# A depthwise convolution and a GRU over 256 steps: another order of channels on the partitions, and what follows from it for loads and products

## The chip, the cores and the metric

The kernel runs on one core of a Trainium2 chip. The metric is the device time of one execution in microseconds, the median of several runs. All times of the profile come from one profiled execution of the kernel before.

## The reference

Inputs: `x` of 16 x 256 x 512 (batch, time, channel), `cond` of 16 x 512, and the weights and biases of a GRU (`W_ih`, `W_hh` of 512 x 1536, gates in the order r, z, n). All is float32.

```
def _L0_cond_ref(x, w):              # causal depthwise convolution, K = 16 taps over time
    return conv_general_dilated(x, w, window_strides=(1,), padding=[(K - 1, 0)],
                                dimension_numbers=('NHC', 'HIO', 'NHC'), feature_group_count=C)

def cell(h, x):                      # GRU step, scanned over 256 steps
    gi = x @ W_ih + b_ih;  gh = h @ W_hh + b_hh
    r = sigmoid(i_r + h_r);  z = sigmoid(i_z + h_z)
    n = tanh(i_n + r * h_n)
    return (1 - z) * n + z * h

x = x + _L0_cond_ref(x, cond[:, None, :])        # x1; cond is the convolution's weight
out = x1 + scan(cell, initial_state=cond, x1)    # the states of all steps are added to x1
```

So `cond` serves as the 16 taps of the convolution and as the GRU's first state. The 256 steps of the GRU depend on each other; the products `x1 @ W_ih` do not.

## The kernel before

**Layout.** A channel c (0 to 511) lies on partition p = 32j + l in slot q, with j = c // 128, and within that block of 128 channels q = column // 32 and l = column % 32: `by_part` cuts 128 columns as `(q l)`. State, `x1T`, `xT` and `ni` stand in this transposed form [128, 4, ...]; the recurrent products put the gates into the natural form, with row 32j + batch and 128 columns of block j, and VectorE turns them back with transposes of 32x32 blocks (`rnT` L449, `zp` L461, `xT` L222, the output at L522), reading or writing 32 neighbouring columns for one block.

**Loads.** `load_weights` (L171 to L178) fetches a gate's 512 x 512 weights (for r and z of `W_ih` 512 x 1024) by four transfers, each to the 32 partitions of one j. Two queues, SP and POOL, issue them, after the two first chunks of x. The weights of the recurrent products (`whh`, gates R, N, Z) are issued last (L579 to L582).

**Start.** TensorE clears banks (`mark`, L350 and L351: bf16 products on the full array), then runs `PAD` = 108 idle products of 32 columns and one moving column (L356), and drains. Of chunk 0 (16 steps of x), slots q = 2 and 3 are convolved on TensorE by 16 products each with a diagonal matrix that ScalarE makes (`conv_on_tensor`, L288 to L300; 128 stationary columns, float32), and slots 0 and 1 on VectorE tap by tap (L265). Then come the biases (`spread_biases`, L362), the candidate's x1 products for the first 8 steps (`ni_units`, L320), r and z's x1 products for the first two steps (`pair_units`, L383), and part of chunk 1's taps on VectorE (`bulk.run(0, HEAD)`).

**A step** (`step`, L403 on) issues on TensorE, in this order: 16 products for r (L418, tile `prz`), 16 for n (L418, `pnh`), 16 for z (L418, `prz`), then `other_products`: two units of `pair_units` (8 products, moving 256 columns) and two units of `ni_units` (8 products). All of these have 16 or 32 stationary columns and go to one of four column groups of the array, j = 0 to 3; the four of a kc run side by side. A float32 product is recorded as two instructions in the profile. Of one unit of `ni_units` the before kernel says:

```
for j in range(NQ):
    nc.tensor.matmul(
        hold[q][32 * j : 32 * j + 32, 0:n],
        lhsT=wih_n[:, kc, j * P + q * L : j * P + q * L + L],
        rhs=x1T[c][:, kc, o : o + n], ...
```

One block of 8 steps has 16 such units, spread over the 8 steps before it. Beside that the other engines make the step's chain: r's sigmoid on ScalarE (L435), `rn` (L447), `rnT` (L449), `n` (L451) on VectorE, tanh on ScalarE (L459), `zp` (L461), sigmoid of z (L465), the difference (L467) and a scan (L474) that writes the new state `hist` for the next step's products for r. VectorE also does the taps of later chunks (L265), as many in each step as a plan (`Plan`, due steps and costs) asks, and the sums for the output.

The changed kernel's line numbers are lower by 3 to 12: its products of the step stand at L413, those of `ni_units` at L316.

Of the kernel before, what the change touches and what calls it, by code (L numbers as in the profile page):

```python
# [24 lines left out]
F32 = mybir.dt.float32  # L25
BF16 = mybir.dt.bfloat16
AF = mybir.ActivationFunctionType
# [3 lines left out]
P = 128  # L31
# [3 lines left out]
CHUNKS = (16,) * 16  # L35
PAD = 108
HEAD = 11.0
SYNC = mybir.DependencyInfo(mybir.DependencyClass.Sync, mybir.DependencyReason.DATA)
# [37 lines left out]
def conv_gru_kernel(  # L76
# [36 lines left out]
    def by_part(natural):  # L113
        return natural.rearrange("p (q l) -> p q l", q=NQ)

# [24 lines left out]
    for j in range(NQ):  # L140
# [12 lines left out]
    nc.vector.memset(ones, 1.0)  # L153
    bn_nat = const.tile([P, P], F32)
    nc.vector.memset(bn_nat, 0.0)

    load_x(1, ((nc.sync,), (nc.gpsimd,)))
    nc.sync.dma_start(out=b_two[0:1, :], in_=b_hh.rearrange("(o c) -> o c", o=1))
    nc.sync.dma_start(
        out=b_two[1:2, 0 : 2 * C], in_=b_ih[0 : 2 * C].rearrange("(o c) -> o c", o=1)  # L160
    )
    nc.gpsimd.dma_start(
        out=bn_nat[0:P:L, :], in_=b_ih[2 * C : 3 * C].rearrange("(j c) -> j c", j=NQ)
    )

# [4 lines left out]

    def load_weights(w_sb, w, g, queues):  # L171
        for j in (0, 2, 1, 3):
            queues[j].dma_start(
                out=w_sb[L * j : L * j + L],
                in_=w[j * P : (j + 1) * P, g * C : g * C + w_sb.shape[2]].rearrange(
                    "(q l) c -> l q c", l=L
                ),
            )  # L178


    for tile_of, g in ((wih_n, N), (wih_rz, R)):
        load_weights(tile_of, w_ih, g, (nc.sync, nc.sync, nc.gpsimd, nc.gpsimd))
    zero_z = [const.tile([P, NQ * B * 2], F32, name=f"zero_z_{i}") for i in range(2)]
# [11 lines left out]
    bnT = const.tile([P, NQ, L], F32)  # L195

# [15 lines left out]
    def turn_units(c):  # L212

        def halo():
            xT[c] = xtp.tile([P, NQ, HALO + CMAX], F32, tag="xT", name=f"xT_{c}")
            if c:
                m = CHUNKS[c - 1] * B
                nc.scalar.copy(xT[c][:, :, 0:HALO], xT[c - 1][:, :, m : m + HALO])

        def turn(a):  # L220
            o = HALO + a * PAIR
            nc.vector.transpose(  # L222
                xT[c][:, :, o : o + GT * B].rearrange("p q (a r) -> p a q r", r=L),
                x_nat[c][:, a : a + GP].rearrange("p a (q l) -> p a q l", q=NQ),
            )
# [79 lines left out]
    def ni_units(t0, steps):  # L305
# [6 lines left out]
        def prod(q, kc):  # L312
# [4 lines left out]
            if kc == 0:  # L317
                hold[q] = ps_ni.tile([P, NI * B], F32, tag="pni", name=f"pni_{t0}_{q}")
            for j in range(NQ):
                nc.tensor.matmul(  # L320
                    hold[q][32 * j : 32 * j + 32, 0:n],
                    lhsT=wih_n[:, kc, j * P + q * L : j * P + q * L + L],
                    rhs=x1T[c][:, kc, o : o + n],
                    start=(kc == 0),
                    stop=(kc == NQ - 1),
                    skip_group_check=True,
                )
            if kc == NQ - 1:
                evictions.append(lambda: evict(q))

        def evict(q):
            nc.scalar.activation(  # L332
                hold["ni"][:, q, 0:n], hold[q][:, 0:n], AF.Identity, bias=bnT[:, q, 0:1]
            )
# [18 lines left out]
    def idle_products(n):  # L353

        for _ in range(n):
            nc.tensor.matmul(  # L356
                spare[0:L, 0, 0:1], lhsT=blank[:, 0:L], rhs=blank[:, 0:1], start=True, stop=True
            )
# [136 lines left out]
    def out_units(g, a0=0, a1=GP, steps=(0, 1), queues=(nc.sync,)):  # L495
# [24 lines left out]
        def store():  # L520
            t = op.tile([P, GP, P], F32, tag="o", name=f"o_{g}_{a0}_{steps[0]}")
            nc.vector.transpose(  # L522
                t[:, 0:w].rearrange("p a (q l) -> p a q l", q=NQ),
                hold["s"][:, 0:w],
# [27 lines left out]
    for q in range(NQ):  # L552
        if q not in Q_PE:
# [3 lines left out]
                last1[:, q : q + 1],  # L557
            )
    conv_on_tensor()

    taps = [fn for i, (_, fn) in reversed(list(enumerate(tap_units(0)))) if i % NQ not in Q_PE]
    needed = (NI - 1) * (NQ - len(Q_PE))
    for fn in taps[:needed]:
        fn()
    for _, fn in turn_units(1):
        fn()
    nc.vector.transpose(bnT, by_part(bn_nat))
    for fn in taps[needed:]:
        fn()
    evictions.pop(0)()  # L570
    first_terms(1)
    give_firsts()
    evictions.pop(0)()
    spread_biases()
    nc.scalar.copy(b_rows, spare)
    seed_rz(0)
    seed_nh(0)
    seed_rz(1)
    for g in (R, N, Z):  # L579

        second = nc.sync if g == Z else nc.gpsimd
        load_weights(whh[g], w_hh, g, (nc.sync, second, nc.gpsimd, nc.gpsimd))  # L582
    for fn in ni_units(*blocks[0]):
# [7 lines left out]
    for c in range(1, NCH):  # L591
        due = starts[c] - NI
        taps = tap_units(c)
# [12 lines left out]
    for t in range(T):  # L606
# [6 lines left out]
        def other_products():  # L613

            for units in (of_pair, of_block):
                for _ in range(2):
                    if units:
                        units.pop(0)()
# [54 lines left out]
```

## Time and profile before

| | |
|---|---|
| median of 3 runs | 1043.28 us (1041.05, 1043.28, 1046.07) |
| span of the profiled execution | 1039.8 us |
| PE (TensorE matmul) busy | 1022.6 us, 98% |
| DVE (VectorE) busy | 926.8 us, 89% |
| ACT (ScalarE) busy | 380.3 us, 37% |
| first recurrent product, and that of the second step | 27.95 us, 36.33 us |
| one step of the GRU, once it runs | 3.92 us |
| moved by DMA in the first 36 us | 7.45 MB |

The profiled execution has no time of its own beside its span; the median of the runs stands 3.5 us above that span, and this is taken for what lies around it.

The chain of waits follows the execution back from its last instruction and says which work ended last at each point. Groups give, for all instructions of one line and shape, the count, the busy time, the mean duration of one and the idle time before them. The timeline lists instructions in order of time; neighbours of one group are merged, so that a row gives the start of the first, the time to the end of the last, and how many. Ends of matmuls are modelled: a matmul of 128 moving columns is drawn with 273 ns, though another can start 27 ns after it. The pace of TensorE is therefore read from starts, not from durations. PEld is the loading of weights into the array, which normally runs ahead of the product that needs it.

### The profile page before, as it was taken

The numbers are of one execution on the slowest core, as the hardware profiler recorded it, in microseconds if no ns is written. First come the engines' busy times: TensorE is split into PE (matmuls) and PEld (weight loads), VectorE is DVE, ScalarE is ACT, GpSimd is POOL, SyncE is SP. The second block draws the span as 40 slices with busy tenths as digits, with TensorE's granted clock in tenths as the row PEclk, the third lists the DMA queues.
The fourth block names the chain that finished last, engine by engine and source line by source line (L and its number), as shares of the span: only waits on it lengthen the run. The fifth ranks groups of instructions, "written<-read, shape, count | busy, mean of one in ns | idle before, by whom it ended". The sixth has DMA issues, their size and how long they took to land.

```text
span 1039.8 us, 71852 instructions
## 1 busy us (share of the span) xinstructions
PE 1022.6 (98%) x32952; PEld 928.5 (89%) x32952; DVE 926.8 (89%) x3606; ACT 380.3 (37%) x1520; POOL 12.4 (1%) x29
## 2 busy tenths in 40 slices
PE   7899999999999999999999999999999999999997
PEld 6699999999999999999999999999999999999986
DVE  7899999999999999999999999999999999896555
ACT  6233433334333333433334333343433334333332
POOL 4000000000000000000000000000000000000000
PEclk9999999999999999999999999999999999999999
DMA  9420101101010010100100010010000000000000
GB/s 216 111 58 13 26 15 29 21 15 31 8 35 14 15 35 8 32 15 19 30 14 26 14 34 15 15 34 5 15 14 15 15 13 6 15 15 15 14 11 17
DMA packets 40850, 27.72 MB, mean 27 GB/s; under 512 B 6686, under 2 KB 38498, under 8 KB 40548
## 3 DMA queue, kind: packets, MB, share of 16 engines
q1 hardware_dynamic: 38756, 18.78, 8.0%
q8 instruction: 257, 4.21, 1.7%
q0 software_dynamic: 1376, 4.20, 1.7%
q14 instruction: 45, 0.37, 0.1%
q10 hardware_dynamic: 416, 0.16, 0.1%
HBM read 14.73 MB, written 8.39 MB: 22 GB/s over the span
## 4 chain that ended last, share of the span: by engine, by line
PE 95%; DMA 3%; DVE 1%; SPq 0%; issue 0%; ACT 0%; DVEq 0%; ACTq 0%
PE prz L418 42%; PE pnh L418 21%; PE prz L383 20%; PE pni L320 10%; DMA whh<-in_L_cond_W_hh_dram 2%; DMA x_nat<-in_x_dram 1%; DVE rnT L449 0%; DVE zp L461 0%; DVE rn L447 0%; SPq L125 0%; ACT zero_z L465 0%; DVE n L451 0%; DMA out_dram<-o 0%; DVE hist L474 0%; DVE glance L398 0%
## 5 line engine op out<-in xcount | busy, mean ns | idle before, releaser
L418 PE MATMUL prz<-whh,hist 128*32 128x128 f32 x16320 | 539.9, 273 | 3.0 <-DVE hist L474 2.1
L418 PEld LDWEIGHTS prz<-whh,hist 128*32 128x32 f32 x16320 | 450.0, 103 | 8.5 <-DVE hist L474 6.6
L265 DVE SCALAR_TENSOR_TENSOR x1T<-xT,condT,x1T 128x256 f32<-128x256 f32 (+2 forms) x930 | 377.4, 462 | 0.0
L418 PE MATMUL pnh<-whh,hist 128*32 128x128 f32 x8160 | 269.7, 273 | 0.0
L383 PE MATMUL prz<-wih_rz,x1T 128*32 128x256 f32 x4096 | 268.2, 379 | 0.1
L418 PEld LDWEIGHTS pnh<-whh,hist 128*32 128x32 f32 x8160 | 226.7, 104 | 0.0
L459 ACT ACTIVATE dn<-n 128x64 f32<-128x64 f32 x256 | 67.9, 265 | 325.9 <-DVE n L451 325.9
L383 PEld LDWEIGHTS prz<-wih_rz,x1T 128*32 128x32 f32 x4096 | 129.0, 110 | 43.7 <-issue 0.3
L320 PEld LDWEIGHTS pni<-x1T,wih_n 128*32 128x32 f32 x4096 | 122.8, 110 | 42.7 <-ACT x1T L300 0.6
L435 ACT ACTIVATE r<-prz 128x128 f32<-128x128 f32 x256 | 71.1, 278 | 238.6 <-PE prz L418 235.5
L320 PE MATMUL pni<-x1T,wih_n 128*32 128x128 f32 x4096 | 158.1, 273 | 0.0
L474 DVE TENSOR_TENSOR_SCAN hist<-zero_z,dn 128x32 f32<-128x32 f32 (+1 forms) x768 | 128.6, 216 | 0.0
L447 DVE TENSOR_TENSOR rn<-r,pnh 128x128 f32<-128x128 f32 x256 | 72.4, 283 | 38.5 <-PE pnh L418 37.2
L465 ACT ACTIVATE zero_z<-zp 128x32 f32<-128x32 f32 x512 | 90.6, 226 | 8.6 <-DVE zp L461 1.8
L449 DVE STREAM_TRANSPOSE rnT<-rn 128x128 f32<-128x128 f32 x256 | 79.7, 311 | 8.7
L461 DVE STREAM_TRANSPOSE zp<-prz 128x128 f32<-128x128 f32 x256 | 80.9, 316 | 1.8 <-PE prz L418 1.7
L332 ACT ACTIVATE ni<-pni,bnT 128x128 f32<-128x128 f32 x128 | 47.1, 368 | 74.7 <-PE pni L320 74.7
L467 DVE TENSOR_TENSOR dn<-hist,dn 128x64 f32<-128x64 f32 x255 | 58.4, 229 | 11.3
L451 DVE TENSOR_TENSOR n<-rnT,ni 128x64 f32<-128x64 f32 x256 | 57.7, 225 | 8.9
L398 DVE COPY glance<-r 1x1 f32<-1x1 f32 x256 | 34.0, 133 | 25.3 <-ACT r L435 25.3
L371 ACT COPY prz<-b_rows 128x256 f32<-128x256 f32 x128 | 48.5, 379 | 0.0
L398 DVE COPY glance<-zero_z 1x1 f32<-1x1 f32 x256 | 36.3, 142 | 8.0 <-ACT zero_z L465 0.3
(51 smaller groups left out, 211.1 us busy)
## 6 DMA issues: line engine op xcount, KB each, us to landing
out_dram<-o SPq DMA_DIRECT2D x248, 32.0 KB, 1.7
x_nat<-in_x_dram SPq DMA_DIRECT2D x118, 64.0 KB, 3.0
whh<-in_L_cond_W_hh_dram POOLq DMA_DIRECT2D x8, 256.0 KB, 14.7
wih_rz<-in_L_cond_W_ih_dram POOLq DMA_DIRECT2D x2, 512.0 KB, 10.2
wih_rz<-in_L_cond_W_ih_dram SPq DMA_DIRECT2D x2, 512.0 KB, 14.3
whh<-in_L_cond_W_hh_dram SPq DMA_DIRECT2D x4, 256.0 KB, 19.0
x_nat<-in_x_dram POOLq DMA_DIRECT2D x8, 64.0 KB, 5.4
wih_n<-in_L_cond_W_ih_dram POOLq DMA_DIRECT2D x2, 256.0 KB, 7.7
```

The costliest lines, as they stand in the source:

```text
L265: nc.vector.scalar_tensor_tensor(out=x1T[c][:, q, to], in0=xT[c][:, q, k * B + to.start : k * B + n], scalar=condT[:, q, k : k + 1], in1=x ...
L320: nc.tensor.matmul(hold[q][32 * j : 32 * j + 32, 0:n], lhsT=wih_n[:, kc, j * P + q * L : j * P + q * L + L], rhs=x1T[c][:, kc, o : o + n], ...
L383: nc.tensor.matmul(rz[p % 2][32 * j : 32 * j + 32], lhsT=x1T[c][:, kc, o : o + PAIR], rhs=w_rz[:, :, j * P : (j + 1) * P], start=False, st ...
L398: nc.vector.tensor_copy(glances[i][0:1], of_scalar[0:1, 0:1])
L418: product = nc.tensor.matmul(dst[32 * j : 32 * j + m], lhsT=h[0](kc), rhs=whh[g][:, kc, j * P : (j + 1) * P], start=False, stop=(kc == NQ ...
L435: of_r = nc.scalar.activation(r, pr, AF.Sigmoid)
L447: nc.vector.tensor_mul(rn, r, pnh)
L449: nc.vector.transpose(rnT, by_part(rn))
L459: nc.scalar.activation(dn_v[:, :, :, 1], n, AF.Tanh)
L461: nc.vector.transpose(zp, by_part(pz))
L465: nc.scalar.activation(z_v[:, qs, :, 1], zp[:, qs, half], AF.Sigmoid) for qs in halves
L474: nc.vector.tensor_tensor_scan(hist_g[:, lo + at : lo + end], z[:, to], dn[:, to], 0.0, op0=ALU.mult, op1=ALU.add,)
```

## The change

Channel 4p + q lies on partition p in slot q: `by_part` cuts 128 columns as `(l q)`, so a 32x32 block to transpose takes every fourth column. With it:

- `load_weights` fetches a gate by two transfers of all 128 partitions, slots 0 and 1 by SP and 2 and 3 by POOL; `whh` is issued right after `W_ih`, and chunk 1 of x after the candidate's weights. The candidate's bias comes by one transfer in place of a load and a transpose.
- A unit of `ni_units` is one product with 128 stationary columns, every fourth of `wih_n`, on the full array, in place of four with 32.
- The idle products are 200 with 40 moving columns (108 with one before); `spread_biases` and the seeds come before the convolution, and chunk 0's taps on VectorE are no longer interrupted by the turn of chunk 1.
- `HEAD` is 7.0 instead of 11.0, chunk 1 is due two steps later, and the units for steps 16 to 23 begin two steps later.

```diff
-PAD = 108
-HEAD = 11.0
+PAD = 200
+IDLE = 40
+HEAD = 7.0
...
     def by_part(natural):
-        return natural.rearrange("p (q l) -> p q l", q=NQ)
+        return natural.rearrange("p (l q) -> p q l", q=NQ)
...
-    load_x(1, ((nc.sync,), (nc.gpsimd,)))
...
+    nc.sync.dma_start(out=bnT, in_=b_ih[2 * C : 3 * C].rearrange("(p q) -> p q", q=NQ))
...
-    def load_weights(w_sb, w, g, queues):
-        for j in (0, 2, 1, 3):
-            queues[j].dma_start(
-                out=w_sb[L * j : L * j + L],
-                in_=w[j * P : (j + 1) * P, g * C : g * C + w_sb.shape[2]].rearrange(
-                    "(q l) c -> l q c", l=L
-                ),
-            )
-
-    for tile_of, g in ((wih_n, N), (wih_rz, R)):
-        load_weights(tile_of, w_ih, g, (nc.sync, nc.sync, nc.gpsimd, nc.gpsimd))
+    def load_weights(w_sb, w, g):
+        rows = w.rearrange("(p q) c -> p q c", q=NQ)
+        for queue, qs in ((nc.sync, slice(0, NQ // 2)), (nc.gpsimd, slice(NQ // 2, NQ))):
+            queue.dma_start(
+                out=w_sb[:, qs], in_=rows[:, qs, g * C : g * C + w_sb.shape[2]]
+            )
+
+    load_weights(wih_n, w_ih, N)
+    load_x(1, ((nc.sync,), (nc.gpsimd,)))
+    load_weights(wih_rz, w_ih, R)
+    for g in (R, N, Z):
+        load_weights(whh[g], w_hh, g)
...
-                x_nat[c][:, a : a + GP].rearrange("p a (q l) -> p a q l", q=NQ),
+                x_nat[c][:, a : a + GP].rearrange("p a (l q) -> p a q l", q=NQ),
...
-            for j in range(NQ):
-                nc.tensor.matmul(
-                    hold[q][32 * j : 32 * j + 32, 0:n],
-                    lhsT=wih_n[:, kc, j * P + q * L : j * P + q * L + L],
-                    rhs=x1T[c][:, kc, o : o + n],
-                    start=(kc == 0),
-                    stop=(kc == NQ - 1),
-                    skip_group_check=True,
-                )
+            nc.tensor.matmul(
+                hold[q][:, 0:n],
+                lhsT=wih_n[:, kc, q:C:NQ],
+                rhs=x1T[c][:, kc, o : o + n],
+                start=(kc == 0),
+                stop=(kc == NQ - 1),
+            )
...
-                spare[0:L, 0, 0:1], lhsT=blank[:, 0:L], rhs=blank[:, 0:1], start=True, stop=True
+                spare[0:L, 0, 0:IDLE], lhsT=blank[:, 0:L], rhs=blank[:, 0:IDLE], start=True, stop=True
...
-                t[:, 0:w].rearrange("p a (q l) -> p a q l", q=NQ),
+                t[:, 0:w].rearrange("p a (l q) -> p a q l", q=NQ),
...
+    spread_biases()
     conv_on_tensor()
-
-    taps = [fn for i, (_, fn) in reversed(list(enumerate(tap_units(0)))) if i % NQ not in Q_PE]
-    needed = (NI - 1) * (NQ - len(Q_PE))
-    for fn in taps[:needed]:
-        fn()
-    for _, fn in turn_units(1):
-        fn()
-    nc.vector.transpose(bnT, by_part(bn_nat))
-    for fn in taps[needed:]:
-        fn()
-    evictions.pop(0)()
-    first_terms(1)
-    give_firsts()
-    evictions.pop(0)()
-    spread_biases()
     nc.scalar.copy(b_rows, spare)
     seed_rz(0)
     seed_nh(0)
     seed_rz(1)
-    for g in (R, N, Z):
-        second = nc.sync if g == Z else nc.gpsimd
-        load_weights(whh[g], w_hh, g, (nc.sync, second, nc.gpsimd, nc.gpsimd))
+    taps = [fn for i, (_, fn) in reversed(list(enumerate(tap_units(0)))) if i % NQ not in Q_PE]
+    for fn in taps:
+        fn()
+    for _, fn in turn_units(1):
+        fn()
+    while evictions:
+        evictions.pop(0)()
+    first_terms(1)
+    give_firsts()
...
-        due = starts[c] - NI
+        due = starts[c] - NI + (2 if c == 1 else 0)
...
             for units in (of_pair, of_block):
-                for _ in range(2):
+                late_block = units is of_block and t // NI == 1
+                for _ in range(((0, 0, 2, 2, 3, 3, 3, 3)[t % NI]) if late_block else 2):
```

More of the change, by code (lines that the diff above doesn't have):

```diff
@@ L153, in conv_gru_kernel @@
     nc.vector.memset(ones, 1.0)
-    bn_nat = const.tile([P, P], F32)
-    nc.vector.memset(bn_nat, 0.0)
-    load_x(1, ((nc.sync,), (nc.gpsimd,)))
+    bnT = const.tile([P, NQ], F32)
     nc.sync.dma_start(out=b_two[0:1, :], in_=b_hh.rearrange("(o c) -> o c", o=1))
@@ L161, in conv_gru_kernel @@
     )
-    nc.gpsimd.dma_start(
-        out=bn_nat[0:P:L, :], in_=b_ih[2 * C : 3 * C].rearrange("(j c) -> j c", j=NQ)
-    )
+    nc.sync.dma_start(out=bnT, in_=b_ih[2 * C : 3 * C].rearrange("(p q) -> p q", q=NQ))
     wih_rz = const.tile([P, NQ, 2 * C], F32)
@@ L193, in prepare_cond @@
         nc.vector.tensor_scalar_add(last1, condT[:, :, K - 1], 1.0)
-    bnT = const.tile([P, NQ, L], F32)
     b_rows = const.tile([P, 3, P], F32)
@@ L332, in evict @@
             nc.scalar.activation(
-                hold["ni"][:, q, 0:n], hold[q][:, 0:n], AF.Identity, bias=bnT[:, q, 0:1]
+                hold["ni"][:, q, 0:n], hold[q][:, 0:n], AF.Identity, bias=bnT[:, q : q + 1]
             )
```

## The prediction

> **What bounds the kernel now.** First the page's shares of busy time and the chain of waits:
>
> ```profile
> PE 1022.6 (98%) x32952; PEld 928.5 (89%) x32952; DVE 926.8 (89%) x3606; ACT 380.3 (37%) x1520; POOL 12.4 (1%) x29
> PE 95%; DMA 3%; DVE 1%; SPq 0%; issue 0%; ACT 0%; DVEq 0%; ACTq 0%
> ```
>
> A busy PE alone proves little, since its ends are modelled, but the chain stays on PE for 95% of the span. Only the start differs: there the chain lies on DMA. The second question is how far the steps' other chain (VectorE, ScalarE) is behind. Two steps in the timeline tell it, one in the middle and one of the last eight, which have no candidate's x1 products (L320):
>
> ```profile
> 500.81 1.06 PE L418 MATMUL prz<-whh,hist 128*32 128x128 f32 x32
> 501.68 1.05 PE L383 MATMUL prz<-wih_rz,x1T 128*32 128x256 f32 x16
> 502.55 0.62 PE L320 MATMUL pni<-x1T,wih_n 128*32 128x128 f32 x16
> 502.62 0.50 DVE L474 TENSOR_TENSOR_SCAN hist<-zero_z,dn 128x32 f32<-128x32 f32 x3
> 502.98 0.29 PE L418 MATMUL prz<-whh,hist 128*16 128x128 f32 x3
> ...
> 1010.59 1.06 PE L418 MATMUL prz<-whh,hist 128*32 128x128 f32 x32
> 1011.47 1.05 PE L383 MATMUL prz<-wih_rz,x1T 128*32 128x256 f32 x16
> 1012.40 0.50 DVE L474 TENSOR_TENSOR_SCAN hist<-zero_z,dn 128x32 f32<-128x32 f32 x3
> 1012.66 0.61 PE L418 MATMUL prz<-whh,hist 128*16 128x128 f32 x13
> ```
>
> From the first product for z to the next step's first for r takes 2.17 us in the middle (0.87 for z, 0.87 for L383, 0.43 for L320, no gap) and 2.07 us at the end, where PE waits for the scan. So the vector chain alone would allow 2.07: it has 0.10 us of slack in a step. If the L320 products cost nothing, 246 steps would gain 246 x 0.10 = 25 us; anything added to them is paid in full.
>
> **The products on the full array.** A step has 8 products now, two groups of four side by side, 0.43 us. It will have two, each of 128 stationary columns. The convolution shows what such products cost in a row:
>
> ```profile
> 18.75 0.48 PE L292 MATMUL conv<-xT,diag 128*128 128x128 f32 x3
> ...
> 19.08 1.31 PEld L292 LDWEIGHTS conv<-xT,diag 128*128 128x128 f32 x11
> ```
>
> Less the last record's 0.26, three records span 0.22: a record each 0.11 us at 128 moving columns. Weight loads come each (1.31 - 0.19) / 10 = 0.112 us. A product is two records, so two products take 4 x 0.109 to 4 x 0.112 = 0.44 to 0.45 us: what they take now. Four column groups side by side already did the work of one full array, and a quarter of the instructions saves no time. I take +1 us over all steps (0 to +3).
>
> **The change of mode.** Before, a step stays with products of one column group throughout. Now L383 and the recurrent products use groups, and the two products between use the full array: two changes in a step. The trace has changes from full to groups, at the start:
>
> ```profile
> 1.72 0.31 PE L351 MATMUL pnh<-blank 128*128 128x128 bf16 x1
> ...
> 1.95 0.10 PEld L356 LDWEIGHTS <-blank 128*32 128x32 bf16 x1 [0.30 <-issue]
> 1.96 0.19 PE L356 MATMUL spare<-blank 128*32 128x1 bf16 x1
> ...
> 20.34 0.26 PE L292 MATMUL conv<-xT,diag 128*128 128x16 f32 x1
> 20.53 0.10 PEld L362 LDWEIGHTS spare<-b_two,ones 2*32 2x32 f32 x1
> 20.53 0.51 PE L362 MATMUL spare<-b_two,ones 2*32 2x384 f32 x1
> ```
>
> Elsewhere a load runs some 0.1 us ahead of its product. Here load and product start together, 0.19 us after the last full product where the pitch was 0.11, and 0.24 us after where it was 0.11: the array emptied first, for 0.08 to 0.13 us. The first product after a late load of 32 columns is drawn 24 ns longer (297 ns against a median of 273 in the answer on line L320). So a change to groups costs 0.08 + 0.02 = 0.10, up to 0.15 us. A change to the full array is not in the trace. The nearest rows bound it: from the same emptying with a covered load, 0.08 + 0.02 = 0.10, to 0.13 with a whole 128-column load in the open, 0.13 + 0.112 = 0.24. I take 0.08 + 0.112 = 0.19, since nothing loads ahead in either row. A gain is excluded: PE has no gap there to fill. Both: 0.29 us in a step, bounds 0.20 and 0.39. There are 30 blocks of 8 steps and one of 6 with such products, 246 steps: **246 x 0.29 = 71 us**, bounds 49 and 96. It is all on the path. The next product for r is queued behind it, and r's sigmoid, `rn` and the scan wait for that. The slack of 0.10 is on the other side: the vector chain becomes later than needed by 0.10 + 0.29 = 0.39 us.
>
> **Every fourth column.** `rnT` and `zp` (L449, L461), the turns of x (L222) and the output's transposes will step by 16 bytes. No DVE row here does; a step of 8 bytes, in the scan's output read by L467, costs nothing visible. 128 columns take 311 ns and 512 take 688: 0.98 ns per element. Unchanged is one bound; twice the rate per element is the other, 128 x 0.98 = 0.13 us for each of two transposes in the step's chain, 0.26 us together. Both lie within the 0.39 us that the slower PE leaves, so I take 0; without that cover they would cost (0.26 - 0.10) x 256 = 41 us. VectorE would be busy for 256 x 0.26 + 31 x 2 x 0.5 = 98 us more, 1025 us of a span of some 1105, still not the bound.
>
> The 128-column loads of `wih_n` step by 16 bytes too. Those of `hist` step by 8 and take 97 to 110 ns like the rest. Bounds: 0, or each load twice as long, 4 x 0.112 = 0.45 us in a step, 246 x 0.45 = 110 us. I take 0, as the nearest row does.
>
> On this the Trainium skill ("SBUF — State Buffer", Door 1: The DMA port swizzle) speaks against the change: SBUF has lines of 16 bytes, and full bandwidth needs at least two accesses to a line. A step of 16 bytes has one; by the rule the transposes and loads would lie near the slow bounds, which adds nothing for the transposes and up to 110 us for the loads. It also says that four float32 can be stepped for free, so it does not decide, and no row here does.
>
> **The start.** The chain waits for the recurrent weights: the first product for z begins at 34.20 us on landing, step 1 at 36.33.
>
> ```profile
> 11.42 22.65 DMA whh<-in_L_cond_W_hh_dram
> ...
> 14.00:21.50 7.50, 7.50 (x68) 6.77 (x70) 7.50 (x28) 3.04 (x8) 1.87 (x4) 1.00 1.03 307
> 21.50:24.00 2.50, 2.50 (x96) 2.30 (x92) 2.50 (x8) 1.97 (x6) 0.33 (x1) 1.00 1.04 211
> ```
>
> The last column is GB/s. The same busy queues move 307 in one stretch and 211 in another, with transfers to 32 partitions. From 9.5 to 34.0 us the table of stages holds 6.25 MB; at 307 GB/s all through that is 20.4 us and ends 4.1 us earlier, at the 344 of the best half microseconds 18.2 us and 6.3 earlier. I take 5; bounds 0 (if packets, not partitions, set the rate) and 6.3. PE follows: convolution done at 20.5 or before, 16 candidate's products by about 23, L383 (1.9 us) by 25, then the first product for r, 2 to 3 us before today's. VectorE follows with `HEAD` = 7: four units fewer in front; the due steps of chunk 1 keep its rate (18.5 units over 10 steps, 14.5 over 8 before).
>
> The idle products: the convolution's first slot took 6.6 us (9.37 to 15.96), the second, of the same sizes, 4.6. Column PEclk stands at 1.00 in both, so by it nothing is to be won; the pitch says that PE ran at half pace until about 13.6 us, after an idle stretch from 5 to 9.4. 200 products of 40 columns close most of that stretch: 2 us less for PE, hidden behind the weights' landing and counted in the 25 us above. The Trainium skill ("TensorE: Matmul & The Clock Gate", Part 1) has the clock halved after about 3.4 us of idleness, which agrees with the pitch and not with the column; by either the sum stays, as DMA ends last. `bnT` in 16-byte pieces, the one-transfer bias and the moved `spread_biases` are small and lie beside the loads: 0.
>
> **Sum.** 1039.8 (span) + 71 + 1 - 5 = 1106.8; with 3.5 around it as between span and median, **1110 us**. Its own bounds: 1043.3 + 49 + 0 - 6 = 1086 and 1043.3 + 96 + 3 = 1142.
>
> **Rivals.**
> 1. *The change of mode costs nothing* inside a stream of ready products; the gaps at the start would be start-up effects (one stands at 2 us, the other falls on two stationary rows too, which is another change). Then steps stay at 3.92 us and the start's gain is left: 1043.3 - 6.3 = 1037, at 5 us 1039. This is the case on the fast side; it decides if both changes together cost under 5 / 246 = 0.02 us. For it: two instances only, none in a step. Against it: two instances, and in both the load was not ahead. 28%.
> 2. *No emptying, but slow transposes*: VectorE's chain becomes the bound, 2.07 + 0.26 = 2.33 us against 2.17: 1043.3 + 41 - 5 = 1079. Nearly the same if only one change of two is paid: 246 x 0.10 = 25, 1063. 19%.
> 3. *The weight loads bind as well*: emptying plus 0.45 us in a step, 1110 + 110 = 1220. 7%.
> 4. Forecast, 1086 to 1142: 46%.
>
> Of rival 1, over three quarters lie under 1038. A measurement of this kernel can tell about 0.5% (5 us) from no change. Chances: faster 0.22, same 0.06, slower 0.72. The range, to hold eight in ten, must reach from rival 1 (with 3 us below it, the spread of the runs shown) over 2 to the forecast's upper bound: 1034 to 1142; the forecast alone is 1086 to 1142.
>
> **What would show it.** Right: in a step of the changed profile, the first L316 product starts some 0.19 us later after L378 than the pitch, with its load beside it and not ahead; the next L413 product 0.10 later; the step takes 4.2 us; PE still carries the chain. Wrong: steps of 3.92 us, and loads of L316 ahead of L378's end. Rival 2 shows as L449 and L461 at 0.44 us and PE waiting for the scan; rival 3 as loads of L316 with a pitch of 0.22 us. For the start: `whh` landed by 29 us, 300 GB/s or more throughout, the convolution's two slots alike at 4.6 us, and step 1 at 31 us.

## The result, and the profile after

The changed kernel takes 1246.8 us (1246.5 to 1246.9, four runs) against 1042.3 us for the kernel before in the same comparison: 1.196 times as long, 95% interval 1.194 to 1.199. The profiled execution took 1246.8 us, its span is 1245.0 us, 205.2 us more than before. That is slower, as forecast, but by three times the forecast's 67 us and outside its range.

The page's shares of busy time and its chain of waits, changed kernel:

```profile
PE 1232.1 (99%) x29972; PEld 1050.3 (84%) x29972; DVE 983.6 (79%) x3604; ACT 371.0 (30%) x1520; POOL 8.9 (1%) x21
PE 97%; DVE 1%; ACT 1%; issue 0%; ACTq 0%; DMA 0%; SPq 0%; DVEq 0%
```

PE issues 9% fewer instructions and is busy 209.5 us longer. Weight loads (PEld) are busy 122 us longer, although the candidate's 4096 loads of 32 columns became 1024 of 128. VectorE's share fell. DMA has left the chain: the start is PE's too.

One step in the timeline (columns: start, us, engine, line, operation, tile, sizes, count; rows that the reading doesn't need are left out, here and below), stationary loads and products:

```profile
599.90 1.05 PE L378 MATMUL prz<-wih_rz,x1T 128*32 128x256 f32 x16
600.88 1.01 PEld L316 LDWEIGHTS pni<-x1T,wih_n 128*128 128x128 f32 x4 [0.41 <-issue]
600.88 1.20 PE L316 MATMUL pni<-x1T,wih_n 128*128 128x128 f32 x4
600.89 0.52 DVE L469 TENSOR_TENSOR_SCAN hist<-zero_z,dn 128x32 f32<-128x32 f32 x3
602.01 1.07 PE L413 MATMUL prz<-whh,hist 128*16 128x128 f32 x32
```

Three things stand here. The first L316 load starts with its product and not ahead of it, after 0.41 us in which the load queue waits for nothing that the profile shows. The scan ends at 601.41, and the next step's products for r start only 0.6 us later (0.61 in the median of the steps): the vector chain no longer decides the end of a step. And the two L316 products, four records, stand from 600.88 to 602.01, 1.13 us, where the eight products took 0.43 us before.

The single records inside that line begin at 600.879, 601.215, 601.450 and 601.683: a pitch of 0.234 us, where contiguous 128-column loads have 0.11 (the convolution, in both kernels). The first distance is 0.336, that is 0.10 more. The last group of four L378 products starts at 600.55 and has streamed by 600.77, if it takes the 0.216 us that lie between the groups before it; by this estimate nothing streams for 0.11 us before the first load. The first L413 record comes 0.327 after the last L316 record, 0.09 more than the pitch.

A step takes 4.755 us in the mean of steps 10 to 245 (from one sigmoid of r to the next), 3.92 before. It splits into 3.49 for r, n, z and L378 as before, 4 x 0.234 = 0.94 for the records of L316, and 0.33 that remains for the two changes of mode (the gaps just read, 0.11 + 0.10 + 0.09, make 0.30 of it). Against before (0.43 for the eight products) that is +0.51 + 0.33; times 246 it is 125 + 81 = 206 us, and the span grew by 205.

### The profile page after: what moved, and what is told of

Read it like the earlier page. It is cut to its first block, busy times and chain, and to the rows that moved or that the text cites. A ratio compares the mean times of both kernels' runs of the same rounds, so it can differ in the third digit from the quotient of the medians.

```text
span 1245.0 us, 65870 instructions
## 1 busy us (share of the span) xinstructions
PE 1232.1 (99%) x29972; PEld 1050.3 (84%) x29972; DVE 983.6 (79%) x3604; ACT 371.0 (30%) x1520; POOL 8.9 (1%) x21
## 4 chain that ended last, share of the span: by engine, by line
PE 97%; DVE 1%; ACT 1%; issue 0%; ACTq 0%; DMA 0%; SPq 0%; DVEq 0%
PE prz L413 38%; PE pni L316 23%; PE pnh L413 18%; PE prz L378 17%; PE conv L289 1%; ACT diag L285 0%; DVE rnT L444 0%; DVE rn L442 0%; ACT dn L454 0%; DVE n L446 0%; DVE dn L462 0%; DVE hist L469 0%; DVE o L517 0%; DVE x1T L262 0%; DMA out_dram<-o 0%
## 5 line engine op out<-in xcount | busy, mean ns | idle before, releaser
L413 PE MATMUL prz<-whh,hist 128*32 128x128 f32 x16320 | 543.8, 274 | 4.5 <-DVE hist L469 4.5
L413 PEld LDWEIGHTS prz<-whh,hist 128*32 128x32 f32 x16320 | 430.3, 103 | 39.0 <-DVE hist L469 8.9
L316 PEld LDWEIGHTS pni<-x1T,wih_n 128*128 128x128 f32 x1024 | 257.6, 324 | 101.3 <-issue 100.9
L316 PE MATMUL pni<-x1T,wih_n 128*128 128x128 f32 x1024 | 304.8, 422 | 0.0
L413 PE MATMUL pnh<-whh,hist 128*32 128x128 f32 x8160 | 269.5, 273 | 0.0
L378 PE MATMUL prz<-wih_rz,x1T 128*32 128x256 f32 x4096 | 267.8, 379 | 0.0
L413 PEld LDWEIGHTS pnh<-whh,hist 128*32 128x32 f32 x8160 | 226.4, 104 | 0.0
L378 PEld LDWEIGHTS prz<-wih_rz,x1T 128*32 128x32 f32 x4096 | 127.9, 110 | 44.1
L469 DVE TENSOR_TENSOR_SCAN hist<-zero_z,dn 128x32 f32<-128x32 f32 (+1 forms) x768 | 131.9, 227 | 0.0
L444 DVE STREAM_TRANSPOSE rnT<-rn 128x128 f32<-128x128 f32 x256 | 108.6, 424 | 8.8
L219 DVE STREAM_TRANSPOSE xT<-x_nat 128x512 f32<-128x512 f32 x32 | 36.4, 1144 | 5.0 <-DMA x_nat<-in_x_dram 5.0
```

Of the source, the lines that this page charges most:

```text
L316: nc.tensor.matmul(hold[q][:, 0:n], lhsT=wih_n[:, kc, q:C:NQ], rhs=x1T[c][:, kc, o : o + n], start=(kc == 0), stop=(kc == NQ - 1),)
L378: nc.tensor.matmul(rz[p % 2][32 * j : 32 * j + 32], lhsT=x1T[c][:, kc, o : o + PAIR], rhs=w_rz[:, :, j * P : (j + 1) * P], start=False, st ...
L413: product = nc.tensor.matmul(dst[32 * j : 32 * j + m], lhsT=h[0](kc), rhs=whh[g][:, kc, j * P : (j + 1) * P], start=False, stop=(kc == NQ ...
L444: nc.vector.transpose(rnT, by_part(rn))
L469: nc.vector.tensor_tensor_scan(hist_g[:, lo + at : lo + end], z[:, to], dn[:, to], 0.0, op0=ALU.mult, op1=ALU.add,)
```

## The experiments

All times are compared with the kernel before on the same chip (1042 to 1044 us). In the short diffs, "after" is the changed kernel.

**1. Contiguous loads on the full array.** Theory A: stationary loads that step by 16 bytes take twice as long and set the pitch. Theory B: on the full array load and product take turns, whatever the step.

```
+    wih_np = const.tile([P, NQ, NQ, P], F32)
+    for kc in range(NQ):
+        nc.gpsimd.tensor_copy(wih_np[:, kc], wih_n[:, kc].rearrange("p (m q) -> p q m", q=NQ))
-                lhsT=wih_n[:, kc, q:C:NQ],
+                lhsT=wih_np[:, kc, q],
```

> The changed kernel, but GpSimd copies the candidate's weights once, at the start, so that the 128 columns of each load of the full-array products lie side by side. Theory A (every load of 128 columns at a step of 16 bytes takes twice as long and sets the pace; beside that the array empties at both changes of mode): the pitch of the records falls from 0.234 to 0.11 us, four of them save 0.37 to 0.48 us in a step, a step falls from 4.75 to 4.3 us, the time from 1247 to 1130 to 1155 us. Theory B (the step of 16 bytes costs nothing; on the full array in this place load and product simply follow each other, 0.112 + 0.109 = 0.22): the pitch stays at 0.23 and the time at 1247, within 5 us.

Measured: 1128.2 us, ratio 1.081 (1.077 to 1.085). The timeline of a step:

```profile
501.12 1.05 PE L381 MATMUL prz<-wih_rz,x1T 128*32 128x256 f32 x16
502.09 0.52 PEld L319 LDWEIGHTS pni<-x1T,wih_np 128*128 128x128 f32 x4 [0.41 <-issue]
502.10 0.71 PE L319 MATMUL pni<-x1T,wih_np 128*128 128x128 f32 x4
502.74 1.07 PE L416 MATMUL prz<-whh,hist 128*16 128x128 f32 x32
```

The four records now stand from 502.10 to 502.74, 0.64 us instead of 1.13, and their pitch is 0.112. The load still starts with its product after the same 0.41 us. The step is 4.263 us. So the copy alone takes back 119 us: A holds (the time is 2 us below its range), B falls. What is left is 86 us over before: 84 in the steps (246 x 0.34; 5 of them because four records take 0.02 us longer than the eight products did, the rest the two changes of mode), and 1.4 because step 1 starts later.

**2. Four column groups instead of the full array, loads still stepped.**

```
+            for j in range(NQ):
                 nc.tensor.matmul(
-                hold[q][:, 0:n],
-                lhsT=wih_n[:, kc, q:C:NQ],
+                hold[q][32 * j : 32 * j + 32, 0:n],
+                lhsT=wih_n[:, kc, j * P + q : (j + 1) * P : NQ],
```

> The changed kernel, but each full-array product is again four products of 32 columns in four column groups; the loads still step by 16 bytes, the rest of the layout stays. Theory A: no changes of mode; if the stepped loads of the four groups share one way in, 16 loads at twice the 27 ns pitch make the 0.44 us stretch 0.87 us, 1150 us; if each group has its own, the stretch stays at 0.44 to 0.5 us, 1040 to 1060 us. Theory B: the full array was all of it, the stretch is 0.44 us again, and the time 1040 to 1050 us, with VectorE's longer transpose (424 against 311 ns) as the only difference in a step.

Measured: 1064.3 us, 1.020 (1.017 to 1.022). The stretch of the products is as forecast, the time is above both forecasts. A step in the timeline, and the group of the loads:

```profile
502.07 0.59 PEld L317 LDWEIGHTS pni<-x1T,wih_n 128*32 128x32 f32 x16
502.14 0.31 DVE L458 STREAM_TRANSPOSE zp<-prz 128x128 f32<-128x128 f32 x1
502.28 0.62 PE L317 MATMUL pni<-x1T,wih_n 128*32 128x128 f32 x16
502.56 0.23 DVE L464 TENSOR_TENSOR dn<-hist,dn 128x64 f32<-128x64 f32 x1
502.82 0.52 DVE L471 TENSOR_TENSOR_SCAN hist<-zero_z,dn 128x32 f32<-128x32 f32 x3
503.10 0.81 PEld L415 LDWEIGHTS prz<-whh,hist 128*32 128x32 f32 x32 [0.44 <-DVE hist L471]
503.10 1.08 PE L415 MATMUL prz<-whh,hist 128*32 128x128 f32 x32 [0.20 <-DVE hist L471]
```

```profile
L317 PEld LDWEIGHTS pni<-x1T,wih_n 128*32 128x32 f32 x4096 | 135.1, 136 | 38.9 <-ACT ni L329 3.2
```

The loads run ahead again (0.21 us before the products), and the group of products is as long as before, 0.62. Each load is drawn longer, 136 ns against 110, which costs PE nothing here. So both losses need the full array, and 182 of the change's 204 us are gone. But now PE waits for the scan, and the chain of waits lies on VectorE for 42%:

```profile
PE 49%; DVE 42%; ACT 4%; DMA 2%; issue 2%; SPq 1%; DVEq 0%; ACTq 0%
```

The 22 us that stay (24 with the 2.3 that this kernel's start gains) are put down to the vector chain, which the slower PE had covered; experiments 6 and 11 test that.

**3. Groups and contiguous loads.** The copy of experiment 1 on top of experiment 2 (`lhsT=wih_np[:, kc, q, L * j : L * j + L]`).

> The changed kernel with both undone for these products: four column groups, and weights copied once so that loads read neighbouring columns. Both theories: 0.44 us in the stretch, steps at 3.92 to 3.95 us (the vector chain is longer by the transpose's 0.11 us and uses up the 0.10 us of slack), 1040 to 1050 us. What is then left against the kernel before is the start and the transposes alone.

Measured: 1067.3 us, 1.023 (1.020 to 1.025): a miss. The steps are 4.016 us, against 4.018 in experiment 2, and the copy makes the first step 3.5 us later. So the step of the loads costs nothing here. As the scan binds in both, this alone would not prove much; the better witness is experiment 11, whose loads step by 16 bytes too and whose steps, bound by PE, are as short as before. With contiguous loads in both, full array against groups is 1128.2 - 1067.3 = 61 us; it is less than 246 x 0.33 = 81 because in the groups' version the vector chain binds.

**4. Four units in every second step**, so that half as many changes of mode are made.

```
-                for _ in range(((0, 0, 2, 2, 3, 3, 3, 3)[t % NI]) if late_block else 2):
+                counts = (0, 0, 0, 4, 0, 4, 0, 8) if late_block else (0, 4) * 4
+                for _ in range(counts[t % NI] if units is of_block else 2):
```

> The changed kernel, but four units of the candidate's x1 products in every second step instead of two in each: as many loads and products, half as many changes of mode (about 124 pairs instead of 246). Theory A with E for one pair of changes: the time falls by 123 x E; with E = 0.3 to 0.45 us by 37 to 55 us, to 1192 to 1210 us. If changes of mode cost nothing and all is paid per load or product: 1247 us, unchanged.

Measured: 1255.9 us, 1.203 (1.199 to 1.208): a miss, slower than the change itself. Two steps in the timeline:

```profile
600.21 1.08 PE L413 MATMUL prz<-whh,hist 128*32 128x128 f32 x32 [0.20 <-DVE hist L469]
...
603.83 1.94 PEld L316 LDWEIGHTS pni<-x1T,wih_n 128*128 128x128 f32 x8 [0.41 <-issue]
603.84 2.13 PE L316 MATMUL pni<-x1T,wih_n 128*128 128x128 f32 x8
...
605.90 1.07 PE L413 MATMUL prz<-whh,hist 128*16 128x128 f32 x32
...
609.78 0.97 PE L413 MATMUL prz<-whh,hist 128*32 128x128 f32 x28 [0.20 <-DVE hist L469]
```

The step with units takes 605.90 - 600.21 = 5.69 us, the one without 3.88, together 9.57; two steps of the change take 9.51. The step with units has room for one pair of changes only: 3.49 + 8 x 0.234 + 0.33 = 5.69. So one pair is saved in two steps, 0.33 us. But the step without units waits for the scan: 3.88 instead of the 3.49 that its products take, 0.39 lost. The saving is real, and what it saves is lost again where PE now has to wait for the vector chain.

**5. The full array in the layout of before**, loads contiguous through the same copy, nothing stepped anywhere.

```
+            nc.gpsimd.tensor_copy(
+                wih_np[:, kc].rearrange("p q (j l) -> p q j l", l=L),
+                wih_n[:, kc].rearrange("p (j q l) -> p q j l", q=NQ, l=L),
+            )
-            for j in range(NQ):
-                    lhsT=wih_n[:, kc, j * P + q * L : j * P + q * L + L],
+                lhsT=wih_np[:, kc, q],
```

> The kernel before, with its own layout and loads, but the candidate's x1 products on the full array; the weights for them are copied once by GpSimd so that a load's 128 columns lie side by side (the copies wait for the weights and may delay the first step by some us). Theory A: the changes of mode alone, 0.33 us in a step as the run with copied weights showed on the other layout, 246 x 0.33 = 81 us: 1120 to 1132 us, with steps of 4.25 us. Rival: in the other layout part of the 0.33 us belonged to VectorE's longer transposes or to something else of the new layout; then the step is clearly under 4.25 us, and the time under 1110.

Measured: 1135.6 us, 1.087 (1.084 to 1.090), steps of 4.260 us, pitch 0.112. The time is 4 us above theory A's range, since the first steps come 11 us later: the copies wait behind the loads. The end of a step:

```profile
600.38 0.52 PEld L327 LDWEIGHTS pni<-x1T,wih_np 128*128 128x128 f32 x4 [0.41 <-issue]
600.38 0.71 PE L327 MATMUL pni<-x1T,wih_np 128*128 128x128 f32 x4
601.02 1.08 PE L424 MATMUL prz<-whh,hist 128*32 128x128 f32 x32
```

The four records stand for 0.64 us, as in experiment 1. A step is 0.34 us longer than before (4.26 - 3.92); 0.02 of that is the records' own, and 0.32 is the pair of changes of mode. So it costs the same in this layout, where no product steps its operands and no transpose does.

**6. Stepping where it is free.** On top of experiment 2, which leaves 22 us, r's sigmoid and `rn` now take every fourth column while they read PSUM, and write in order, so that `rnT` reads SBUF in order.

```
-        of_r = nc.scalar.activation(r, pr, AF.Sigmoid)
+        of_r = nc.scalar.activation(r.rearrange(by_q, q=NQ), by_part(pr), AF.Sigmoid)
-        nc.vector.tensor_mul(rn, r, pnh)
+        nc.vector.tensor_mul(rn.rearrange(by_q, q=NQ), r.rearrange(by_q, q=NQ), by_part(pnh))
```

> The changed kernel with four column groups (stepped loads), and the step of 16 bytes moved in the chain from a read of SBUF to reads of PSUM: ScalarE reads r's sums and VectorE n's sums by every fourth column and write them side by side, so that rnT is read side by side. Theory A (a step of 16 bytes costs in SBUF and not in PSUM; what is left of the layout, 22 us, is VectorE's time): rnT at 311 ns again, rn and r as before, steps shorter where VectorE was late, 1045 to 1056 us. Rival (PSUM reads at that step cost as much on ScalarE or in rn): r at 0.35 to 0.4 us or rn at 0.4 us, and 1062 us or more.

Measured: 1050.5 us, 1.006 (1.004 to 1.008), as theory A has it. The same groups with the step in SBUF (first fence, experiment 2; columns behind the bar: busy us, mean ns) and in PSUM (second, this kernel):

```profile
L446 DVE STREAM_TRANSPOSE rnT<-rn 128x128 f32<-128x128 f32 x256 | 108.4, 423 | 8.7
L458 DVE STREAM_TRANSPOSE zp<-prz 128x128 f32<-128x128 f32 x256 | 79.0, 308 | 0.0
L219 DVE STREAM_TRANSPOSE xT<-x_nat 128x512 f32<-128x512 f32 x32 | 36.5, 1148 | 5.4 <-DMA x_nat<-in_x_dram 5.4
L519 DVE STREAM_TRANSPOSE o<-sum 128x512 f32<-128x512 f32 x31 | 36.1, 1164 | 0.0
```

```profile
L449 DVE STREAM_TRANSPOSE rnT<-rn 128x128 f32<-128x128 f32 x256 | 79.8, 312 | 8.7
L445 DVE TENSOR_TENSOR rn<-r,pnh 128x128 f32<-128x128 f32 x256 | 71.4, 279 | 32.5 <-PE pnh L415 30.5
L433 ACT ACTIVATE r<-prz 128x128 f32<-128x128 f32 x256 | 71.2, 278 | 240.1 <-PE prz L415 238.7
```

A step of 16 bytes in SBUF makes `rnT` 423 ns instead of 311, and 512 columns 1148 to 1164 instead of 688 to 703. `zp` takes the same step from PSUM in 308, against 316 without it. With the step moved to PSUM, `rn` (279, before 283) and r (278, before 278) pay nothing, and `rnT` is back at 312.

**7. GpSimd puts x and the output in order**, so that the last stepped transposes go too (two `nc.gpsimd.tensor_copy`, one for a chunk of x, one for each piece of the output).

> As the run before it in this list, and the turns of x (from chunk 2) and the output's transposes also read and write neighbouring columns: GpSimd, idle until now, copies x and the output into the other order. Theory A (all that was left of the layout is VectorE's stepped access): steps of 3.92 us, PE on the chain again, 1038 to 1044 us, some 2 us of it from the start. Rival (GpSimd's copies and VectorE get in each other's way): VectorE's operations longer by some per cent, 1050 us or more.

Measured: 1076.2 us, 1.030 (1.028 to 1.032). The rival held, and the way it does so is hidden in the mean. The same group of taps before and here, and a step with one of GpSimd's copies of x:

```profile
L265 DVE SCALAR_TENSOR_TENSOR x1T<-xT,condT,x1T 128x256 f32<-128x256 f32 x900 | 369.4, 466 | 0.0
```

```profile
L271 DVE SCALAR_TENSOR_TENSOR x1T<-xT,condT,x1T 128x256 f32<-128x256 f32 x900 | 409.6, 512 | 0.6 <-ACT x1T L245 0.6
```

```profile
447.82 3.16 DVE L271 SCALAR_TENSOR_TENSOR x1T<-xT,condT,x1T 128x256 f32<-128x256 f32 x3
447.94 2.35 POOL L135 COPY x_perm<-x_nat 128x1024 f32<-128x1024 f32 x1 [14.82 <-DVE xT L226]
```

The taps are not all a tenth slower. In the trace of this run 38 of them take 1.19 to 2.41 us, and no other takes over 0.5. In the step shown the second of the three taps starts at 448.18, inside the copy, and ends at 450.58, 0.29 us after it. So a tap that starts beside a copy lasts until the copy is over. The steps concerned took 4.3 and, for the long copies of x, up to 5.5 us. Transposes beside a copy (`rnT`, `zp`) kept their 311 and 308 ns.

**8. A step of 8 bytes** on the full array: experiment 1 with the copy written two elements apart.

```
-    wih_np = const.tile([P, NQ, NQ, P], F32)
+    wih_np = const.tile([P, NQ, NQ, P, 2], F32)
```

> The changed kernel with full-array products and copied weights, but the copy leaves every second column free, so that a load steps by 8 bytes. If what counts is two columns in 16 bytes, the records' pitch is 0.11 us as with neighbouring columns: 1126 to 1131 us. If every step beyond neighbours costs, 0.23 us as with 16 bytes: 1245 us; in between, in between.

Measured: 1134.9 us, 1.087 (1.084 to 1.089), pitch 0.118 us: 4 us above the first forecast, far from the second. The end of a step:

```profile
500.65 0.74 PE L319 MATMUL pni<-x1T,wih_np 128*128 128x128 f32 x4
501.32 1.08 PE L416 MATMUL prz<-whh,hist 128*32 128x128 f32 x32
```

The four records take 0.67 us, where experiment 1 has 0.64 and the change 1.13. So steps of 4, 8 and 16 bytes give a pitch of 0.112, 0.118 and 0.234: the cost is not proportional to the step, it comes between two elements in 16 bytes and one.

**9. ScalarE puts x and the output in order**, 128 columns at a time, one piece at the end of a step, on top of experiment 6.

> Four column groups, the chain's step on the PSUM side, and the other order of x (from chunk 3) and of the output made by ScalarE in pieces of 128 columns, one in a step after z's sigmoids, where it has some 1 us free. Theory A (what is left of the layout is VectorE's stepped access of SBUF, 0.45 us for each of two transposes in 8 steps, and GpSimd hurt only because its copies slow VectorE): steps of 3.92 to 3.93 us, 1038 to 1043 us. Rival (ScalarE's stepped reads and writes are slow too, or come in the way of r's sigmoid): pieces of 0.4 us or more, r later, 1048 us or more.

Measured: 1044.7 us, 1.0017 (1.0006 to 1.0027): just missed. The steps are 3.942 us in the mean. One in sixteen takes 4.43 (the forecast of experiment 11 says one in eight): there a piece and, once in a chunk, a copy of `xT` of 1.03 us stand ahead of r's sigmoid on ScalarE.

**10. 280 idle products instead of 200** at the start, on top of experiment 6.

> The kernel with four column groups and the chain's step on the PSUM side, and 280 idle products instead of 200, so that TensorE is busy until about 10 us. If the half pace in the convolution comes from the idle stretch before it, no half pace is seen and the first step starts up to 1.5 us earlier, 1049 to 1050 us against 1050.5; if the start waits for VectorE's taps or the loads, the convolution ends earlier and the time is the same.

Measured: 1052.1 us, 1.009 (1.007 to 1.011); no gain over experiment 6's 1050.5. The convolution starts later, at 11.56 us instead of 10.78. And although PE was idle for only 0.8 us between 5 and 11 us, against 1.9 in experiment 6, the column of the granted clock stands at 0.68 from 11 to 13 us and 0.50 from 13 to 15, where it is 1.00 in experiment 6. More idle products do not prevent this; what decides it stays open.

**11. The pieces of experiment 9 behind r's sigmoid**, where ScalarE has nothing to do.

```
             (seed_nh if s else seed_rz)(p + 1)
+            if t < T - 8:
+                give_perm(1)
-        give_perm(1 if t < T - 8 else 99)
+        if t >= T - 8:
+            give_perm()
```

> e10_act with ScalarE's pieces moved from the end of the step to the place right behind r's sigmoid and the bias copy for the next pair, where ScalarE has some 1.2 us without work. Theory (the change's layout costs nothing of itself once its steps of 16 bytes are read from PSUM or copied off the path): the steps take 3.92 us in the mean as before (in e10_act 3.94, with one of 4.42 in eight, where two copies stood ahead of r's sigmoid), the first steps stay some 3 us earlier, and the time is 1038 to 1041 us against 1042.4. Rival (the pieces slow the step wherever they stand, through ScalarE's share of SBUF or through the output they hold back): 1043 to 1046.

Measured: 1040.6 us, 0.998 (0.997 to 0.999), against 1042.4: far faster than the change, and 0.2% faster than the kernel before, little but with an interval that ends below 1. The forecast holds. Its chain of waits, and its transposes of 512 columns:

```profile
PE 92%; DVE 5%; DMA 2%; ACT 1%; issue 0%; ACTq 0%; SPq 0%; DVEq 0%
L566 DVE STREAM_TRANSPOSE oq<-sum 128x512 f32<-128x512 f32 x31 | 20.9, 674 | 0.0
L242 DVE STREAM_TRANSPOSE xT<-x_perm 128x512 f32<-128x512 f32 x26 | 17.8, 687 | 0.0
```

The steps are 3.924 us as before; the sigmoid of step 1 comes at 34.4 us instead of 37.5. It keeps the change's loads and its order of channels; it undoes the full array, and leaves VectorE no step in SBUF but in chunks 0 to 2 of x and the last pieces of the output. Its loads of `wih_n` still step by 16 bytes, and PE, which carries 92% of the chain, pays nothing for it.

**12. Loads to 128 partitions in the layout of before**, one transfer for each slot q; the order in which loads are issued is the changed kernel's too.

```
+        rows = w.rearrange("(j q l) c -> q j l c", q=NQ, l=L)
+        for q, queue in ((0, nc.sync), (2, nc.gpsimd), (1, nc.sync), (3, nc.gpsimd)):
+            queue.dma_start(out=w_sb[:, q], in_=rows[q, :, :, g * C : g * C + w_sb.shape[2]])
```

> The kernel before, with its own layout (nothing steps by 16 bytes), its column groups and its convolution, but each weight load goes to all 128 partitions for one slot (a quarter of each of four blocks of 32 partitions), as the changed kernel's do. Theory (partitions per transfer set the rate; it is the one part of the change that brings something): the recurrent weights land some 3 to 5 us earlier, the candidate's products of block 0 then bind the start, the first z product comes about 3 us earlier, the steps stay at 3.92: 1038 to 1040 us against 1042.4. Rival (the kernel's new order of loads, or the idle products, brought those 3 us, not the partitions): 1041 to 1044, with the recurrent weights landing as late as before.

Measured: 1073.2 us, 1.029 (1.027 to 1.031); both theories missed. Two stretches of the table of stages, after first, then this kernel (last column GB/s):

```profile
14.00:21.50 7.50, 7.50 (x55) 7.42 (x54) 6.49 (x24) 2.60 (x7) 1.06 (x3) 0.95 1.03 351
21.50:24.00 2.50, 2.50 (x12) 2.50 (x13) 1.92 (x5) 2.02 (x6) 0.00 (x0) 1.00 1.02 387
```

```profile
14.00:21.50 7.50, 7.50 (x64) 6.77 (x67) 1.34 (x5) 1.03 (x2) 1.37 (x2) 1.00 0.93 131
21.50:24.00 2.50, 0.85 (x24) 0.43 (x23) 0.00 (x0) 0.00 (x0) 2.36 (x4) 0.86 0.97 144
```

With DMA as busy by its share (0.93 to 1.03), 131 to 144 GB/s are moved instead of 351 to 387 (before: 307 and 211), and the first steps come 30 us later. What is behind that shows plainly later, where SP's issues of the recurrent weights stand. These issues, after and here, and a stretch of the stages here:

```profile
8.97 3.30 SPq L172 DMA_DIRECT2D whh<-in_L_cond_W_hh_dram  x3
13.68 38.19 SPq L174 DMA_DIRECT2D whh<-in_L_cond_W_hh_dram  x6
40.00:50.00 10.00, 3.39 (x36) 1.12 (x32) 2.46 (x7) 0.00 (x0) 0.00 (x0) 0.64 0.27 99
```

The DMA share is down to 0.27 (0.26 from 50 to 60 us), 4 of 16 engines, and the trace has 4 or 5 packets in flight there nearly all the time; in the kernels before and after it has 16 to 18 while the weights come in. A busy engine moves as much as after: 99 / (0.27 x 16) = 23 GB/s, against 387 / (1.02 x 16) = 24. So the engines that work are what is lost. The source of these transfers lies in four blocks of 32 rows. A first version of this kernel, e12_loads, gave no time, but its forecast had this as its rival: if a source of four blocks lets only a part of the DMA engines work, below 200 GB/s and 1055 us or more. That fits, in the rate, the time and the number of engines; a source cut otherwise, which would prove it, was not tried. Open is also why the packets take so long between 14 and 24 us, where some 15 are in flight at a third of the rate.

So 128 partitions alone do not make a load fast. The change's transfers have no such blocks: they bring two neighbouring rows of 2 KB to each partition, 4p and 4p + 1 or 4p + 2 and 4p + 3.

## Why the prediction was right or wrong

- **The step that failed: "I take 0, as the nearest row does".** The 16-byte step of the full array's loads was sized at 0 with bounds of 0 and 110 us. It measured 4 x 0.122 = 0.49 us in a step, 120 us on a path that PE alone carries, and experiment 1 takes back 119. The row taken as nearest, the loads of `hist`, steps by 8 bytes. Experiment 8 shows that 8 bytes cost 6 ns where 16 cost 122: that row lies on the other side of the jump, so "near" in bytes was not near in price. It also has 16 or 32 columns and goes to column groups, where experiment 2 shows that even 16 bytes are free.
- **The rule was waved off.** The prediction said of the Trainium skill ("SBUF — State Buffer", Door 1: The DMA port swizzle) that it did not decide, since it has both "two accesses to a line" and "four float32 for free". The runs agree with the first half: two elements in 16 bytes 0.118 us, one 0.234, and `rnT` 311 to 423 ns. They contradict the second, if it means a step of four float32 in SBUF. With the first half taken at its word the sum would have been 1220 us, which is rival 3.
- **Rival 3 is what happened**: 1220 forecast, 1246.8 measured; its pitch of 0.22 us was 0.234. It got 7%, and the range ended at 1142, because the bound of 110 us was priced as a rival and left out of the forecast's own bounds. A range has to take in the bounds of its own unknown costs; this one was left outside.
- **The change of mode** was sized at 0.29 us a step, bounds 0.20 to 0.39; it is 0.33 (81 us, not 71), by the budget of the step, by experiment 1 and, in another layout, by experiment 5 (0.32). So the mechanism was right, and the size within its bounds; rival 1, which had it cost nothing, is refuted. The emptying and the load in the open are where the prediction put them: 0.11 + 0.10 into the full array, 0.09 back. The Trainium skill states it as well ("TensorEngine Tiling (Array Packing)", Key Properties: a change of the tiling mode drains TensorE); the runs agree, with the 0.33 us.
- **"A quarter of the instructions saves no time", +1 us**: right for contiguous loads; four such records take 0.45 against 0.43.
- **The transposes** were taken as hidden behind the slower PE. In the steps they are: after, the scan ends 0.6 us before PE needs it. Their price was 0.13 us each for `rnT` and `zp`; `rnT` pays 0.11 and `zp`, which reads PSUM, nothing. Without the cover they cost 22 us with all stepped operands (experiment 2), not 41.
- **The start, -5 us, came to nothing.** The recurrent weights do land at about 29 us, as said, at 351 to 387 GB/s from 14 to 24 us (between 9.5 and 14 us it is 213, not the 300 or more that was to hold throughout). But the candidate's first products are full-array products with stepped loads as well, and PE now ends last. From the chain of waits in order of time (start us, us, what), after:

```profile
10.34 10.81 PE conv L289 x64
21.15 7.56 PE pni L316 x32
28.71 1.86 PE prz L378 x32
...
36.42 1.08 PE prz L413 x32
```

  The 32 records of L316 take 7.56 us, 0.236 each, where the groups took 3.84 before; that eats 3.7 of the 5. The convolution also starts 1 us later than before (10.34 against 9.37), in both kernels 0.14 us after the end of the turns of chunk 0, which take 2.10 us with the 16-byte step and 1.30 without: here a stepped transpose is on the path. And its two slots are not alike at 4.6 us: the first takes 6.2, the second 4.5, and the column of the granted clock stands at 0.57 from 11 to 15 us. In experiments 2, 6 and 9, with the same 200 idle products, both slots take 4.5 us; in experiment 11 the first takes 6.0 again. So the 2 us that the idle products were to save on PE come in some of these profiles and not in others. Step 1 starts at 36.42 us, before at 36.33. Without the full array (experiments 2, 6, 9, 11) the start gains 2.3 to 3.1 us: the "2 to 3 us" that the prediction had from PE's own work.
- **Loads to all 128 partitions as the cause of the faster start** was an assumption. Experiment 12 shows that 128 partitions are not enough for it; as its own transfers leave only 4 engines at work from 36 to 60 us, it does not show whether they are needed. What made the change's loads faster than before (351 to 387 GB/s from 14 to 24 us, against 307 and 211) stays open.
- **The 3.5 us around the span** were 1.8 in the profiled execution (1246.8 - 1245.0); the rest was the spread of the runs.

## What to carry to other kernels

Before one takes a nearest row as a price, ask whether it is on the same side of the thing that could bind: here an operand with one float32 in every 16 bytes of SBUF took twice as long where one 128-column load followed the other, and an operand with two took hardly longer than one in order. A bound that cannot be settled belongs in the forecast's range, not only in a rival. When the layout needs a step somewhere, let an engine take it while it reads PSUM, or in small copies by an engine that is idle at that moment (and does not make VectorE wait, as GpSimd did), and keep the products of one loop in one mode of the array: a pair of changes cost a third of a microsecond in every step.

## What the runs showed of the hardware

- Stationary loads of 128 float32 columns on the full array: a pitch of 0.112 us in order, 0.118 with 8 bytes between elements, 0.234 with 16.
- The same 16-byte step in loads of 32 columns to four groups side by side: each drawn 136 ns instead of 110, no time on PE (experiments 2 and 11).
- A pair of changes between column groups and the full array: 0.32 to 0.33 us, with or without stepped operands.
- VectorE's transposes with a 16-byte step in SBUF: 311 to 423 ns (128 columns), 688 to 1148 (512 columns, reading) and 703 to 1164 (writing). Read from PSUM: 316 without that step, 308 with it.
- GpSimd copies of SBUF beside VectorE's float32 taps: 38 of 900 taps took 1.19 to 2.41 us instead of 0.47, until the copy was over; single steps went from 3.9 to 5.5 us.
- Transfers to 128 partitions at 2 KB each, whose source lies in four blocks of 32 rows: from 40 to 60 us 4 of 16 DMA engines at work (share 0.26 to 0.27), 97 to 99 GB/s, 23 GB/s for each.
